# Layer 0 of a two-layer graph network: row sums taken inside the weighted sums, a scatter moved behind the gathers, and layer-norm statistics shared between VectorE and ScalarE

## The chip, the core and the metric

The kernel runs on one core of a Trainium2 chip. A core has five engines that run side by side, each from its own queue of instructions: TensorE (PE, matrix products; its weight loads are listed as PEld), VectorE (DVE), ScalarE (ACT), GpSimd (POOL, which here also issues the indirect DMAs) and SyncE (SP, which issues plain DMAs). The metric is the time of the whole program on the device in microseconds, lower is better.

## The reference

Inputs are 2708 nodes with 1024 features, a 0/1 adjacency matrix and square weights. Cut to what matters:

```python
# layer 0
f, g = x @ Wf + bf, x @ Wg + bg
e    = relu(f @ g.T)
att  = softmax(where(adj > 0, e, -9e15), axis=1)
x    = layernorm(x + att @ (x @ W + bW))
# layer 1
h    = x @ W1
e    = leaky_relu(h @ a1 + (h @ a2).T, 0.2)
att  = softmax(where(adj > 0, e, -9e15), axis=1)
x    = layernorm(x + relu(att @ h))
# layernorm(x) = (x - mean) / sqrt(var + 1e-5), over the 1024 features
```

The adjacency has some 16 neighbours a node, so the kernel never forms a full attention matrix.

## The kernel before

**Preparation (to about 250 us).** The adjacency is read row by row, each row's neighbours are turned into a list of at most 40 indices, and the nodes are sorted by list length into 85 groups of 32. A block is four groups (128 nodes; the first holds one group only). Each node has its list split over four partitions, so that one *tile* is 128 gathered rows: one neighbour for each of four list quarters of 32 nodes. Most blocks of layer 0 have 20 tiles. The products `M = Wf Wg^T` and the vectors derived from the biases are made here, so that a score is one dot product of a neighbour's raw row of x with the row `F = x M + c` of the node.

**Layer 0 (about 250 to 1155 us)** is one loop over blocks, software-pipelined over five of them: while block k is summed, block k+1 is scored, block k+2 gets its `F`, the block before k is multiplied by W, and block k+3 is loaded. In the order in which the loop body emits them, the steps are:

- `replicate(b, k)`: four ScalarE copies spread 32 rows of `F` from PSUM to the 128 partitions of one of four `Fr` buffers; each block needs four of these, sixteen copies of 32x1024.
- `q_dot` (the bias part of the score) and the steps of `close` of the block before: residual sum `z = pm + z`, statistics, `z` normalized in place by one ScalarE instruction, `z` written to `X1S`, two dots of `z` with `u2b` and `u1b`, and `z` with its dot scattered into the table `T1`, which layer 1 gathers from.
- `Layer.sums`: `po += st^T ring`, where `ring` holds the gathered rows and `st` the attention weights. Four column strips of TensorE work at once, one queue of matmuls each. A tile's two halves of 512 columns lie in different strips. When both have been emitted, its ring slot is free and the next gather is emitted on POOL (`gathers`). The ring has 20 slots. The row sums of the softmax are a small matmul of `rs` into a PSUM tile `pt`, of which VectorE takes the reciprocal `ri`; ScalarE scales `po` by it into `y`.
- `x_turn` (transposes of a later block's x), the product with `Wt`, `q_spread`, the product with `M`, and the transposes of `y`. All transposes and the row sums share two rotating `pt` buffers, the products share two `pm` buffers.
- `dots` (one VectorE pass of 1024 columns per tile), then `soft`, which makes `st` and `rs`.

**What sets the order.** Each engine is wrapped in `InOrder`: its instructions are issued exactly in the order in which the loop emits them, and wait for other engines by semaphores. Generators (`close`, `turn`, `q_spread`) are advanced by `next` at chosen places, which is how a step's pieces are interleaved; `hooks` in `sums` let the caller run the rest of `close` after the thirteenth tile. Since all calls go through one wrapper, nearly every line of the profile is that wrapper's, L71; steps are told apart by tile names. The tile called `xT` serves for the transposed y too, and a group `j<-ring,Fr` is one dot.

**Layer 1** gathers rows of `T1`, sums them first, multiplies by `W1`, and closes with the same `norm`.

Of the kernel before, what the change touches and what calls it, by code (L numbers as in the profile page):

```python
# [8 lines left out]
F32 = mybir.dt.float32  # L9
BF16 = mybir.dt.bfloat16  # L10
I32 = mybir.dt.int32
# [95 lines left out]
def listed_path(ctx, tc, x, adj, Wf, bf, Wg, bg, W, bW, W1, a1, a2, out):  # L107
# [39 lines left out]
    make_identity(nc, ident)  # L147
    ones = const.tile([P, 1], F32, name="ones")
    nc.gpsimd.memset(ones, 1.0)
    ones3 = const.tile([35, P], BF16, name="ones3")  # L150
    nc.gpsimd.memset(ones3, 1.0)

    stack = const.tile([P, 32], F32, name="stack")
    rep = const.tile([P, Q, 32], F32, name="rep")
# [16 lines left out]
    f1 = const.tile([P, NB], F32, name="f1")  # L171
    nc.gpsimd.memset(f1, 0.0)
    s0 = const.tile([P, 1], F32, name="s0")
    rows3 = const.tile([35, D], BF16, name="rows3")
    c3, b3 = rows3[0:3], rows3[32:35]
    scores = [const.tile([P, Q, QT], F32, name=f"scores{i}") for i in range(2)]
    for t in scores:
# [357 lines left out]
    def product(n, xT, w, row=None):  # L535


        pm = ps_m.tile([P, H, 512], F32, name="pm")
        for h in range(H):
            half_product(pm, h, n, xT, w, row)  # L540
        return pm

    def half_product(pm, h, n, xT, w, row=None):
        c = slice(h * 512, (h + 1) * 512)
        if row is not None:
            pe.matmul(pm[:n, h, :], ones3[row:row + 3, :n], rows3[row:row + 3, c], start=True, stop=False)
        for k in range(KC):
            pe.matmul(pm[:n, h, :], xT[:, k, :n], w[:, k, c],
                      start=(row is None and k == 0), stop=(k == KC - 1))

    def two_products(n, xT, w, row=None):

        halves = [ps_m.tile([P, H, 512], F32, name="pm") for h in range(H)]
        for h in range(H):
            half_product(halves[h], h, n, xT, w, row)
        return halves

    def split_product(xT, w, parts, row=None, pm=None):

        pm = ps_m.tile([P, H, 512], F32, name="pm") if pm is None else pm
        for h in range(H):
            c = slice(h * 512, (h + 1) * 512)
            if row is not None:
                pe.matmul(pm[:32, h, :], ones3[row:row + 3, :32], rows3[row:row + 3, c], start=True, stop=False)
            for k in range(KC // Q):
                for p in range(Q):
                    i = p * KC // Q + k
                    pe.matmul(pm[32 * p:32 * p + 32, h, :], xT[:, i, :32], w[:, i, c],  # L570
                              start=(k == 0 and (row is None or p > 0)), stop=(k + 1 == KC // Q))
        yield
        act.copy(parts, flat(pm))
        yield
        pm = ps_m.tile([P, H, 512], F32, name="pm")
        for h in range(H):
            pe.matmul(pm[:, h, :], rep, parts[:, h * 512:(h + 1) * 512], start=True, stop=True)
        return pm
# [11 lines left out]
    def scatter(table, idx, src):  # L590
        pool.indirect_dma_start(
            out=table, out_offset=bass.IndirectOffsetOnAxis(ap=idx, axis=0), in_=src,
            in_offset=None, bounds_check=N - 1, oob_is_err=False)

    def norm(z, n, made=None):


        st = small.tile([P, H, 6], F32, name="bst")
        mv = small.tile([P, 2], F32, name="mv")
        for h in range(H):  # L600
            if made is not None:
                made(h)
            dve.bn_stats(st[:n, h, :], z[:n, h * 512:(h + 1) * 512])
        dve.bn_aggr(mv[:n], st[:n])
        var, r, t = (small.tile([P, 1], F32, name=s) for s in ("var", "rstd", "newton"))
        dve.tensor_scalar(var[:n], mv[:n, 1:2], EPS, None, op0=ALU.add)
        ri, ti = r.bitcast(I32), t.bitcast(I32)
        dve.tensor_scalar(ti[:n], var.bitcast(I32)[:n], 1, None, op0=ALU.logical_shift_right)
        dve.tensor_scalar(ri[:n], ti[:n], -1.0, float(0x5F3759DF), op0=ALU.mult, op1=ALU.add)
        for _ in range(3):  # L610
            dve.tensor_scalar(t[:n], var[:n], r[:n], r[:n], op0=ALU.mult, op1=ALU.mult)
            dve.tensor_scalar(t[:n], t[:n], -0.5, 1.5, op0=ALU.mult, op1=ALU.add)
            dve.tensor_scalar(r[:n], r[:n], t[:n], None, op0=ALU.mult)
        sh = small.tile([P, 1], F32, name="sh")
        dve.tensor_scalar(sh[:n], mv[:n, 0:1], r[:n], -1.0, op0=ALU.mult, op1=ALU.mult)
        yield
        act.activation(z[:n, :D], z[:n, :D], AF.Identity, bias=sh[:n], scale=r[:n])
# [24 lines left out]
    class Layer:  # L642
# [57 lines left out]
            u.rs = small.tile([P, Q], F32, name="rs")  # L700
            dve.tensor_reduce(u.rs[:, :u.G], sc, AX.X, ALU.add)

        def sums(self, u, po, hooks, y):

            pt = ps_t.tile([P, 4, P], F32, name="pt")
            place = lambda k, h: 32 * ((k + 2 * h) % 4)
            for h in range(H):  # L710
                for k in range(u.G):
                    j = place(k, h)
                    pe.matmul(pt[j:j + 32, 0, h:h + 1], stack, u.rs[:, k:k + 1], start=True, stop=True)
            ri = small.tile([P, H], F32, name="ri")
            spans = [(slice(0, P), slice(0, H))] if u.G == 4 else \
                [(slice(j, j + 32), slice(h, h + 1)) for h in range(H) for j in (place(0, h),)]
            for rows, h in spans:
                dve.reciprocal(ri[rows, h], pt[rows, 0, h])
            index = {(k, t): m for m, (k, g, t) in enumerate(u.tiles)}

            queues = []
            for c in range(4):
                two = [(k, h) for h, k in enumerate((c, (c + 2) % 4)) if k < u.G]
                queues.append([(k, h, t) for t in range(u.T) for k, h in two if t < TILES[u.gs[k]]])
            done, halves = 0, {}
            while any(queues):
                now = [q.pop(0) for q in queues if q]
                for k, h, t in now:
                    j = place(k, h)
                    pe.matmul(po[j:j + 32, h, :], u.st[:, u.col[k, t], :],  # L730
                              self.rows(u.at + index[k, t])[:, h * 512:(h + 1) * 512],
                              start=(t == 0), stop=(t == TILES[u.gs[k]] - 1))
                for k, h, t in now:
                    halves[k, t] = halves.get((k, t), 0) + 1
                    if halves[k, t] == H:
                        self.free.add(u.at + index[k, t])
                        self.gathers()
                        for f in hooks.get(done, []):
                            f()
                        done += 1  # L740
            for k, fs in sorted(hooks.items()):
                if k >= done:
                    for f in fs:
                        f()
            for h in range(H):
                rows = slice(0, P) if u.G == 4 else slice(place(0, h), place(0, h) + 32)
                c = slice(h * 512, (h + 1) * 512)
                act.activation(y[rows, c], po[rows, h, :], AF.Copy, scale=ri[rows, h:h + 1])
# [107 lines left out]
    with ExitStack() as s0s:  # L856
# [62 lines left out]
        def close(b):  # L919
# [6 lines left out]
                dve.tensor_add(z[:n, c], pm[h][:n, h, :], z[:n, c])  # L926

            if b + 1 < NB:
                dve.tensor_add(z[:n, :D], flat(pm)[:n], z[:n, :D])
            steps = norm(z, n, None if b + 1 < NB else add)  # L930
            next(steps)
            yield
            for _ in steps:
                pass
            sp.dma_start(X1S[start[b]:start[b] + m, :], z[:m, :D])
            yield
            dot(z[:n, :D], u2b, n, z[:n, D:D + 1])
            dot(z[:n, :D], u1b, n, f1[:n, b:b + 1])
            yield
# [72 lines left out]
        for k, u in enumerate(units):  # L1012
# [9 lines left out]
                for _ in yTs[back][1]:  # L1022
                    pass
            reps = list(range(len(nxt.gs))) if nxt is not None and not first else []
            for r in reps[:1]:
                replicate(nxt.b, r)
            next(closing, None)
            if loaded is not None:
                q_dot(loaded)
                loaded = None  # L1030
            next(closing, None)
            for r in reps[1:3]:
                replicate(nxt.b, r)
            if nxt is None:

                for _ in closing:
                    pass
                Wp[back] = product(P, yTs.pop(back)[0], Wt, 32)
            lay.sums(u, po, {12: [lambda s=closing: [None for _ in s]]}, y[b])
            closing = iter(())  # L1040
            if ahead is not None and not first:
                x_turn(ahead)
# [3 lines left out]
            if back is not None and nxt is not None:  # L1046
                load_residual(back)
                if back > 0:
                    Wp[back] = product(P, yTs.pop(back)[0], Wt, 32)
                else:  # L1050
                    Wp[back] = whole(split_product(yTs.pop(back)[0], Wt, frp.tile([P, D], F32, name="Fr"), 32))
            if k + 2 == NB:
                load_residual(b)
            spreading = iter(())
# [16 lines left out]
            if k + 4 < NB and not first:  # L1071
                load_lists(seq[k + 4])
            if nxt is not None:
                dots(nxt, 0, len(nxt.tiles))
            for _ in spreading:
                pass
            if nxt is not None:
# [5 lines left out]
        load_residual(b)  # L1083
        for _ in yTs[b][1]:
            pass
        Wp[b] = two_products(P, yTs.pop(b)[0], Wt, 32)
        for _ in closing:
            pass
        for _ in close(b):
# [521 lines left out]
```

## Time and profile before

| | us |
|---|---|
| median of 3 runs | 1772.31 (1768.69 to 1783.73) |
| the profiled execution, its own time | 1778.06 |
| its span from first to last instruction | 1776.3 |
| PE busy | 1586.4 (89%) |
| DVE busy | 1295.3 (73%) |
| POOL busy | 1188.0 (67%) |
| ACT busy | 643.4 (36%) |
| mean granted TensorE clock | 0.959 |

Every number of a view belongs to the one profiled execution. A line of the timeline gives start, duration (of several merged instructions, from the first's start to the last's end), engine, source line, operation, output<-input names with shapes, and a count; in brackets stands the idle time just before it and what ended that idle time. A mean clock below 1.00 in a stretch is a TensorE that ran part of it at reduced speed. An engine's busy share says little by itself: an engine may be busy because it is the bound, or idle because something in front of it in its own queue waits.

### The profile page before, as it was taken

Reading aid. Unit: us, or ns where it says so; the run is one execution under the profiler, and the core shown is the slowest. Engines: PE = TensorE matmul, PEld = TensorE weight load, DVE = VectorE, ACT = ScalarE, POOL = GpSimd, SP = SyncE. Lnnn points to the kernel's source line nnn. Section 1 sums busy time; section 2 is a strip of 40 time slices with the busy share of each in tenths; the row PEclk is TensorE's granted clock in tenths of the full one; section 3 lists DMA queues with packets and bytes.
Section 4 is the critical chain, followed back from the end, with each engine's and each line's share of the span. In section 5 each row is a group of like instructions: output and inputs, shape, how many; then the busy total and the mean of one; then the engine's idle time right before and its main releaser. Section 6 shows DMA issues by size and latency. Waiting matters only on the chain. (4 is left out here: it accounts for less than half of the span.)

```text
span 1776.3 us, 22882 instructions
## 1 busy us (share of the span) xinstructions
PE 1586.4 (89%) x6969; PEld 677.2 (38%) x6969; DVE 1295.3 (73%) x4262; ACT 643.4 (36%) x902; POOL 1188.0 (67%) x1192
## 2 busy tenths in 40 slices
PE   5999389899999999999999999739899897998896
PEld 3444133343444443443444444313344333343342
DVE  5879756888888888888888887637656556665652
ACT  4545454444444455454555554101111111111111
POOL 8878476467666666667666664167777777777740
PEclk9999789899999999999999999969999999999998
DMA  7646168568777777777787787299999999999960
GB/s 284 245 160 240 44 227 318 207 213 289 291 283 270 264 250 256 272 282 266 277 295 278 268 296 297 88 359 368 365 369 394 392 392 378 383 395 391 391 250 37
DMA packets 149984, 502.79 MB, mean 283 GB/s; under 512 B 32340, under 2 KB 32372, under 8 KB 147144
## 3 DMA queue, kind: packets, MB, share of 16 engines
q0 software_dynamic: 132032, 428.29, 65.3%
q1 hardware_dynamic: 10202, 55.72, 8.4%
q10 hardware_dynamic: 7618, 17.23, 2.7%
q8 instruction: 57, 0.93, 0.2%
q14 instruction: 75, 0.61, 0.1%
HBM read 509.64 MB, written 33.75 MB: 306 GB/s over the span
## 5 line engine op out<-in xcount | busy, mean ns | idle before, releaser
L71 POOL DMA_INDIRECT ring<-in_x_dram,SL x405 | 438.6, 1083 | 253.1 <-issue 91.4
L71 DVE SCALAR_TENSOR_TENSOR j<-ring,Fr 128x1024 bf16<-128x1024 f32 x402 | 494.4, 1230 | 82.5 <-DMA ring<-in_x_dram,SL 55.7
L71 PE MATMUL po<-ring,st 128*32 128x512 f32 x2616 | 322.7, 618 | 47.8 <-ACT y L71 30.4
L71 ACT COPY Fr<-pm 32x1024 f32<-32x1024 f32 (+2 forms) x353 | 340.7, 965 | 21.1 <-PE pm L71 16.4
L71 PE MATMUL pm<-M,yT 128*128 128x512 f32 (+1 forms) x704 | 313.3, 598 | 0.5 <-ACT yT L71 0.5
L71 PE MATMUL pm<-M,xT 128*128 128x512 f32 x672 | 307.2, 611 | 0.0
L71 PE MATMUL pm<-Wt,xT 128*128 128x512 f32 (+1 forms) x704 | 303.5, 599 | 0.0
L71 POOL DMA_INDIRECT ring<-T,SL x249 | 246.9, 992 | 83.3 <-issue 69.9
L71 ACT ACTIVATE scores<-scores 128x12 f32<-128x12 f32 (+9 forms) x65 | 14.0, 216 | 669.3 <-DVE scores L71 669.3
L71 PEld LDWEIGHTS pm<-M,yT 128*128 128x128 f32 (+1 forms) x704 | 127.8, 186 | 184.7 <-issue 183.5
L71 PEld LDWEIGHTS pm<-M,xT 128*128 128x128 f32 x672 | 127.1, 194 | 165.3 <-issue 165.3
L71 PEld LDWEIGHTS po<-ring,st 128*32 128x32 f32 x2616 | 103.8, 114 | 222.9 <-issue 182.3
L71 POOL DMA_INDIRECT more<-T,SL x156 | 154.7, 992 | 47.5 <-issue 40.7
L71 PEld LDWEIGHTS pm<-Wt,xT 128*128 128x128 f32 (+1 forms) x704 | 125.0, 186 | 151.8 <-issue 151.1
L409 POOL TENSOR_TENSOR adj<-adj,iota 128x2708 f32<-128x2708 f32 (+3 forms) x23 | 130.5, 5685 | 24.4 <-ACT adj L71 24.3
L412 DVE MAX8 cand<-adj 128x8 f32<-128x136 f32 (+2 forms) x440 | 97.2, 285 | 35.8 <-POOL adj L409 35.8
L71 PE MATMUL pm<-halfT,WfT 128*128 128x512 f32 x256 | 113.2, 597 | 1.1 <-ACT WfT L71 1.1
L71 POOL DMA_INDIRECT SL<-LD,idq x85 | 86.0, 1011 | 25.8 <-issue 22.4
L71 PE MATMUL po<-more,st 128*32 128x512 f32 x624 | 83.8, 632 | 17.8 <-ACT y L71 17.8
L71 DVE TENSOR_SCALAR scores<-ring,f1q 128x4 f32<-128x4 f32 (+6 forms) x69 | 16.0, 238 | 99.3 <-DMA ring<-T,SL 95.9
L71 PEld LDWEIGHTS pm<-halfT,WfT 128*128 128x128 f32 x256 | 48.0, 192 | 57.4 <-issue 54.7
L71 ACT ACTIVATE y<-po,ri 128x512 f32<-128x512 f32 (+1 forms) x88 | 57.5, 678 | 20.9 <-PE po L71 20.3
(211 smaller groups left out, 1509.0 us busy)
## 6 DMA issues: line engine op xcount, KB each, us to landing
adj<-in_adj_dram SPq DMA_DIRECT2D x21, 1354.0 KB
X1S<-z SPq DMA_DIRECT2D x19, 512.0 KB
ring<-in_x_dram,SL POOLq DMA_INDIRECT x405, 6.6
rows<-in_L_gnn_Wg_dram ACTq DMA_DIRECT2D x8, 512.0 KB
rows<-in_L_gnn_Wf_dram ACTq DMA_DIRECT2D x8, 512.0 KB
rows<-in_L_gnn_W_dram ACTq DMA_DIRECT2D x8, 512.0 KB
Wt<-in_L_gnn_W_dram ACTq DMA_DIRECT2D x1, 4096.0 KB
M<-in_L_gnn_W_dram SPq DMA_DIRECT2D x1, 4096.0 KB
```

The source lines that it names most:

```text
L71: made = self.tc.keep_in_program_order(op(*args, **kwargs))
L409: nc.gpsimd.tensor_tensor(k[:n, cut], k[:n, cut], iota[:n, cut], op=ALU.mult)
L412: nc.vector.max(cand[:n, s, :], k[:n, s * SEG:min((s + 1) * SEG, N)])
```

## The change

Five things change in layer 0, and one of them (the root) in layer 1 as well.

1. *Bias rows.* The bias enters a product as a first matmul. Its operands grow from 3 rows to 128: `rows3` has all 128 partitions, cleared to zero outside the six rows in use, and the constant operand is a column of `pick`, broadcast. The bias matmuls of both halves are emitted ahead of both halves' products.
2. *Row sums within sums.* The matmul of the row sums is emitted after the first four finished tiles, the reciprocal after the last. Two of the four strip queues take their two halves in reverse order.
3. *Scatter behind the gathers.* `hooks` is gone. The rest of `close`, now the scatter alone, is emitted after `sums` and after the first five dots of the next block.
4. *Statistics.* The residual sum also gives the sum of each row (`accum_out`); ScalarE's Square with the mean as its bias gives the sum of squares; `bn_stats` and `bn_aggr` remain for the last block of layer 0 and for layer 1. `rsqrt` has two VectorE operations in a Newton step instead of three.
5. *Order.* The `next(closing)` calls are placed anew around `replicate` and `q_dot`: two `replicate` calls instead of one now stand between the first and the second.

```diff
-    ones3 = const.tile([35, P], BF16, name="ones3")
-    nc.gpsimd.memset(ones3, 1.0)
+    pick = const.tile([P, 2], BF16, name="pick")
+    nc.gpsimd.memset(pick, 0.0)
+    nc.gpsimd.memset(pick[0:3, 0:1], 1.0)
+    nc.gpsimd.memset(pick[32:35, 1:2], 1.0)
...
-    rows3 = const.tile([35, D], BF16, name="rows3")
+    rows3 = const.tile([P, D], BF16, name="rows3")
+    nc.gpsimd.memset(rows3, 0.0)
...
         for h in range(H):
+            bias_row(pm, h, n, row)
+        for h in range(H):
             half_product(pm, h, n, xT, w, row)
         return pm
 
+    def bias_row(pm, h, n, row):
+        pe.matmul(pm[:n, h, :], pick[:, row:row + 1].to_broadcast([P, n]), rows3[:, h * 512:(h + 1) * 512], start=True, stop=False)
...
-        if row is not None:
-            pe.matmul(pm[:n, h, :], ones3[row:row + 3, :n], rows3[row:row + 3, c], start=True, stop=False)
...
+    def rsqrt(v, n, scale):
+        half, r, t = (small.tile([P, 1], F32, name=s) for s in ("half", "rstd", "newton"))
+        dve.tensor_scalar(half[:n], v, 0.5 * scale, 0.5 * EPS, op0=ALU.mult, op1=ALU.add)
+        ri, ti = r.bitcast(I32), t.bitcast(I32)
+        dve.tensor_scalar(ti[:n], half.bitcast(I32)[:n], 1, None, op0=ALU.logical_shift_right)
+        dve.tensor_scalar(ri[:n], ti[:n], -1.0, float(0x5F3759DF - 0x400000 - (1 << 31)), op0=ALU.mult, op1=ALU.add)
+        for _ in range(3):
+            dve.tensor_scalar(t[:n], half[:n], r[:n], r[:n], op0=ALU.mult, op1=ALU.mult)
+            dve.tensor_scalar(r[:n], t[:n], 1.5, r[:n], op0=ALU.subtract, op1=ALU.mult)
+        return r
...
-        def sums(self, u, po, hooks, y):
-            pt = ps_t.tile([P, 4, P], F32, name="pt")
+        def sums(self, u, po, y):
             place = lambda k, h: 32 * ((k + 2 * h) % 4)
-            for h in range(H):
-                for k in range(u.G):
-                    j = place(k, h)
-                    pe.matmul(pt[j:j + 32, 0, h:h + 1], stack, u.rs[:, k:k + 1], start=True, stop=True)
-            ri = small.tile([P, H], F32, name="ri")
...
+            def totals():
+                pt = ps_t.tile([P, 4, P], F32, name="pt")
+                for h in range(H):
+                    for k in range(u.G):
+                        j = place(k, h)
+                        pe.matmul(pt[j:j + 32, 0, h:h + 1], stack, u.rs[:, k:k + 1], start=True, stop=True)
+                return pt
...
                 two = [(k, h) for h, k in enumerate((c, (c + 2) % 4)) if k < u.G]
+                if c > 1:
+                    two.reverse()
...
             while any(queues):
+                if pt is None and done >= min(4, u.T):
+                    pt = totals()
...
-                        for f in hooks.get(done, []):
-                            f()
                         done += 1
...
+            if pt is None:
+                pt = totals()
+            ri = small.tile([P, H], F32, name="ri")
...
             if b + 1 < NB:
-                dve.tensor_add(z[:n, :D], flat(pm)[:n], z[:n, :D])
-            steps = norm(z, n, None if b + 1 < NB else add)
-            next(steps)
-            yield
-            for _ in steps:
-                pass
+                mean, ss, sh = (small.tile([P, 1], F32, name=s) for s in ("mean", "ss", "sh"))
+                dve.scalar_tensor_tensor(z[:n, :D], flat(pm)[:n], 1.0, z[:n, :D], op0=ALU.mult, op1=ALU.add,
+                                         accum_out=mean[:n])
+                dve.tensor_scalar(mean[:n], mean[:n], -1.0 / D, None, op0=ALU.mult)
+                yield
+                act.activation(flat(pm)[:n], z[:n, :D], AF.Square, bias=mean[:n], accum_out=ss[:n])
+                yield
+                r = rsqrt(ss[:n], n, 1.0 / D)
+                dve.tensor_scalar(sh[:n], mean[:n], r[:n], None, op0=ALU.mult)
+                yield
+                act.activation(z[:n, :D], z[:n, :D], AF.Identity, bias=sh[:n], scale=r[:n])
...
             sp.dma_start(X1S[start[b]:start[b] + m, :], z[:m, :D])
-            yield
             dot(z[:n, :D], u2b, n, z[:n, D:D + 1])
             dot(z[:n, :D], u1b, n, f1[:n, b:b + 1])
             yield
...
-            for r in reps[:1]:
+            next(closing, None)
+            for r in reps[:2]:
                 replicate(nxt.b, r)
-            next(closing, None)
             if loaded is not None:
                 q_dot(loaded)
                 loaded = None
             next(closing, None)
-            for r in reps[1:3]:
+            next(closing, None)
+            for r in reps[2:3]:
                 replicate(nxt.b, r)
...
-            lay.sums(u, po, {12: [lambda s=closing: [None for _ in s]]}, y[b])
+            lay.sums(u, po, y[b])
+            early = min(5, len(nxt.tiles)) if nxt is not None else 0
+            if nxt is not None and not first:
+                dots(nxt, 0, early)
+            else:
+                early = 0
+            for _ in closing:
+                pass
...
             if nxt is not None:
-                dots(nxt, 0, len(nxt.tiles))
+                dots(nxt, early, len(nxt.tiles))
```

## The prediction

> **What bounds the kernel now.** I read the windows first, to find the stretch that the diff touches. Layer 0's steady blocks run from 369.2 to 1083.5 us:
>
> ```profile
> 369.20:1083.50 714.30, 690.94 (x3082) 293.64 (x3082) 623.50 (x1404) 353.05 (x426) 477.81 (x446) 1.00 0.76 271
> ```
>
> Columns: PE, PEld, DVE, ACT, POOL busy us, granted clock, DMA share, GB/s. TensorE is busy for 97% of it at full clock. The stretch holds 17 blocks, 42.0 us each. Then the timeline of one block by engine, TensorE first:
>
> ```profile
> 661.20 1.04 PE L71 MATMUL pt<-ident,y 128*128 128x128 f32 x8
> 664.17 0.29 PE L71 MATMUL pt<-rs,stack 128*32 128x1 f32 x14 [1.94 <-ACT xT L71]
> ...
> 664.33 8.76 PE L71 MATMUL po<-ring,st 128*32 128x512 f32 x79
> 673.02 1.37 PE L71 MATMUL pt<-ident,xb 128*128 128x128 f32 x8
> 674.32 0.39 PE L71 MATMUL pm<-rows,ones 3*128 3x512 bf16 x1
> ```
>
> The order is y's transposes, row sums, weighted sums, x's transposes, the W product, the M product. TensorE pauses once, 1.94 us ahead of the row sums. Over 400 to 1000 us the waits list 12.0 us (8 times, for ACT xT) and 8.4 us (6 times, for DVE rs) there: 20.4/14 = 1.5 us a block. So about 40.6 us is TensorE's own floor. Now ScalarE and VectorE in the same block:
>
> ```profile
> 662.79 0.22 ACT L71 ACTIVATE scores<-scores 128x24 f32<-128x24 f32 x1 [19.91 <-DVE scores L71]
> 663.04 1.14 ACT L71 COPY xT<-pt 128x512 f32<-128x512 f32 x3
> 664.05 4.04 ACT L71 COPY Fr<-pm 32x1024 f32<-32x1024 f32 x4
> 669.82 1.24 ACT L71 ACTIVATE z<-z,sh,rstd 128x1024 f32<-128x1024 f32 x1 [1.73 <-DVE sh L71]
> 671.09 8.12 ACT L71 COPY Fr<-pm 32x1024 f32<-32x1024 f32 x8
> ```
> ```profile
> 663.94 1.21 DVE L71 TENSOR_TENSOR z<-pm,z 128x1024 f32<-128x1024 f32 x1
> ...
> 669.57 0.21 DVE L71 TENSOR_SCALAR sh<-mv,rstd 128x1 f32<-128x1 f32 x1
> 669.70 1.22 DVE L71 SCALAR_TENSOR_TENSOR j<-xb,rb 128x1024 bf16<-128x1024 f32 x1
> ...
> 671.10 1.22 DVE L71 SCALAR_TENSOR_TENSOR j<-z,u2b 128x1024 bf16<-128x1024 f32 x1
> ...
> 673.51 0.16 DVE L71 RECIPROCAL ri<-pt 128x2 f32<-128x2 f32 x1
> 673.63 1.22 DVE L71 SCALAR_TENSOR_TENSOR j<-ring,Fr 128x1024 bf16<-128x1024 f32 x1
> ```
>
> z is normalized behind four Fr copies, eight follow. The reciprocal sits behind the two dots over z. x's second four transposes need the PSUM buffer that it frees (two pt buffers rotate): 673.51 lets the bias matmul start at 674.32, 0.81 later. Who waits for ri is small today:
>
> ```profile
>   PEld pt L71: 6.5, 16
> ```
>
> The reciprocal lands just as the sums end. That is the tight joint of this schedule.
>
> **What the Trainium skill says.** "TensorE: Matmul & The Clock Gate", section "Architectural detail", calls ScalarE and VectorE strict FIFOs. The trace agrees: at 671.10 the dot starts 0.04 us after z ends, and the dots over ring follow it only. The same page, "What's actually happening", says that idleness in a free-running window of 3413 ns halves the array's clock. The trace shows both outcomes after short pauses: 2.10 us before 707.01 was followed by
>
> ```profile
> 708.00:712.00 4.00, 4.00 (x32) 1.28 (x27) 3.55 (x14) 2.76 (x3) 0.99 (x1) 0.66 0.02 4
> ```
>
> (clock 0.66, sums of 10.46 instead of 8.76 us); 3.11 us before 835.45 was not. "ScalarE: Activation LUTs", section "Table sets", warns that a function outside the loaded set costs a load; this trace has one load of 1.283 us in all, and Square is not in it.
>
> **The change, part by part.** I write E for the end of y's transposes and R for the start of the reciprocal. By the compiled instruction order, ScalarE's new order is Exp, three y copies, Square, *eight* Fr copies, z, four Fr copies, y. VectorE's is sum-add, mean, q dot, root, two dots over z, reciprocal, dots over ring. So "dots first" does not put the ring's dots ahead of z's, and z moves from behind four copies to behind eight.
>
> *From R to the next E (TensorE).* Today 0.81 to the bias, then 674.32 to 704.91 = 30.59 for both products and y's transposes: 31.4 us. Bias rows: each takes 0.32 us start to start (631.65 to 631.97), four a block. With 128 rows and loads grouped by product I bound them between -0.4 and +0.4 us a block, from 128x128 loads at 0.19 against 0.09 us on one side and hidden loads on the other; I take -0.2. E = R + 31.2.
>
> *From E to the next R (ScalarE, then VectorE).* Copies of yT end 0.8 after E (619.93+1.04 against 620.62+1.14). Square: like z, 1.24, plus an accumulator read of 0.19 (the row of adj): 1.43. Writing to PSUM may make it 1.0 to 1.3; I keep 1.24. Eight copies 8.12. z 1.24 and two hops, 1.3. The two dots 2.42 (628.43 to 630.85). Sum 0.8+1.43+8.12+1.3+2.42 = 14.1.
>
> Period 31.2 + 14.1 = 45.3 us. The row sums no longer hold the weighted sums, but those end well inside the 14.1: 9.1 with the totals, 0.7 for half of x's transposes, then TensorE waits 14.1 + 0.3 - 9.8 = 4.6 us, *in every block*. That is longer than the clock's window. One window at half clock loses at most 1.7 us of products directly on this path; part of the window falls in the pause. I take 1.4, ends 0 and 3.4. Period 46.7.
>
> *VectorE's own loop* is shorter: 20 dots x 1.272 = 25.4, soft 3.9, sum-add with its read and mean 1.6, then Square to R without the y copies 13.3 plus the reciprocal and a hop 0.2: 44.4. Either loop alone is over 42.
>
> *Statistics.* From z's sum to sh is 4.6 us on VectorE now (665.16 to 669.78). New: 0.1 read, 0.2 mean, three setup operations 0.56, six Newton operations of 0.31, sh 0.2 = 2.9; 1.7 us saved, but it ends about seven us before z's turn on ScalarE. Worth nothing while the copies stand in front; without them it would come back as 1.7 a block. Layer 1's root saves 0.4 on its last block only.
>
> *Gathers.* Reversing two of the four queues finishes tiles 0 and 1 after one round (0.85 us) instead of two, so the first gather comes 0.85 earlier; the scatter (1.3 us of POOL) no longer stands among them. VectorE waits 52.5 us for ring DMAs in layer 0 (65 times), about 3 a block; those go. Covered: dots start at E + 14.3, and gather m lands at E + 1.2 + 1.35m + 6.7, always earlier.
>
> *The scatter behind the gathers* stands before xb, z and four SL loads on POOL. Twenty gathers end at E + 28.2; scatter landing takes 8.2 us, and the residual z, in the same buffer, waits for it, then issues and lands in 5.9: E + 43.6 with the issue gaps. The sum-add needs it by E + 46.0 to keep Square behind the y copies. Hidden by 2.4 us; in a 43 us block it would be next in line. SL loads end by E + 44, before the next gathers.
>
> *Start.* Clearing rows3 on POOL is at most 1 us (128x484 f32 took 0.49), and POOL idles 2.02 us at 8.7: nothing. *The first and last blocks:* the first reciprocal moves from 334.5 to 340.3 by the same sum, but TensorE waits there for Fr copies anyway, leaving 2.1 us at the next E and R at 385.1 instead of 377.3: +7.8. Sixteen periods to 1051.8 (42.15 now): 16 x (46.7 - 42.15) = +72.8. To the next sums +0.8. At the end the last reciprocal but one delays y by 2.5. Layer 1 (1159.7 to the end) keeps its 616.6 us.
>
> Sum: 7.8 + 72.8 + 0.8 + 2.5 = +84 us. Against its own run the profiled time 1778.1 (span 1776.3) becomes 1862. The median of runs, 1772.3, is 0.3% under that execution: **1856 us**.
>
> **The rivals.**
> (a) *The stall without the clock loss.* Period 45.3: 7.8 + 50.4 + 3.3 = +62, 1834. For it: the 3.11 us pause left the clock alone. Against: 4.6 us can't miss a window as those did.
> (b) *Faster.* ScalarE's queue is not what ends last: the copies of Fr finish early enough, the reciprocal comes by the end of the sums, and TensorE's pause of 1.5 us vanishes. Decides where E to R falls under 9.8. 17 x 1.5 + 17 x 0.2 = -29: 1743. For it: 97% busy and a pause that goes. Against: eight copies alone are 8.12.
> (c) *No difference,* 1772: what the copies add and the vanished DMA waits cancel, were the TensorE wait hidden by a changed rotation of buffers. The compiled order keeps VectorE's wait on x's second transposes.
> (d) *Worse still.* Square displaces Exp's set: two loads of 1.28 us a block (2.66 each by the skill's section "What ACT_TABLE_LOAD costs"), on ScalarE's part of the path: 17 x 2.6 to 17 x 5.3, +44 to +90 more, 1900 to 1946. Its main evidence against is that Identity, Copy, Relu and Exp already share one load.
>
> **How the numbers follow.** Main case 0.58, (a) 0.24, (b) 0.06, (c) 0.04, (d) 0.08. Faster or slower by 1% (18 us) is about what this measurement can tell. Main case with its ends: bias +-0.4 and clock 0.8 to 2.2 a block give 1840 to 1875; with (a) and its bias bound the low end is 1825, and a part of (d) or a second clock window takes the high end to 1882. (b), (c) and most of (d) stay outside. Slower 0.90, same 0.04, faster 0.06.
>
> **What would show it.** Reciprocals 46.7 us apart; TensorE waiting 4 to 5 us for ri before x's second transposes in each block; clock below 1.00 after it; the dot over z waiting 6 us or more for ACT z; no DVE wait for ring DMAs; scatter after the twentieth gather; layer 1 as long as before. I am wrong if z's Identity runs ahead of the copies, if x's transposes don't wait, or if a table load stands beside Square.

## The result and the profile after

The changed kernel takes 1849.05 us (median of 4 runs, 1846.37 to 1851.21); the kernel before, run beside it, 1773.95 (4 runs). The ratio is 1.040, with a 95% interval from 1.037 to 1.043 (the two medians alone give 1.042). The profiled execution took 1847.13 us, with a span of 1845.3 against 1776.3 before: 69.0 us more.

The steady stretch of layer 0 again, in the same window of time as before (PE, PEld, DVE, ACT, POOL busy us, clock, DMA share, GB/s):

```profile
369.20:1083.50 714.30, 643.77 (x2806) 281.42 (x2799) 550.10 (x1209) 346.00 (x425) 437.55 (x423) 0.94 0.70 253
```

TensorE's busy time in it has dropped from 690.94 to 643.77 us, and the clock from full to 0.94. The timeline of two blocks on TensorE, with the weighted sums left out, shows both losses:

```profile
696.21 0.66 PE L71 MATMUL pt<-ident,xb 128*128 128x128 f32 x4
701.21 1.01 PE L71 MATMUL pt<-ident,xb 128*128 128x128 f32 x4 [4.34 <-DVE ri L71]
702.01 1.06 PE L71 MATMUL pm<-rows,pick 128*128 128x512 bf16 x2
702.87 14.85 PE L71 MATMUL pm<-Wt,xT 128*128 128x512 f32 x32
717.55 0.28 PE L71 MATMUL pt<-qd,rep 128*128 128x4 f32 x2
717.69 0.59 PE L71 MATMUL pm<-rows,pick 128*128 128x512 bf16 x2
718.12 13.89 PE L71 MATMUL pm<-M,xT 128*128 128x512 f32 x32
731.86 1.04 PE L71 MATMUL pt<-ident,y 128*128 128x128 f32 x8
...
746.68 1.11 PE L71 MATMUL pt<-ident,xb 128*128 128x128 f32 x4 [4.35 <-DVE ri L71]
747.58 1.06 PE L71 MATMUL pm<-rows,pick 128*128 128x512 bf16 x2
748.44 15.95 PE L71 MATMUL pm<-Wt,xT 128*128 128x512 f32 x32
```

Between the halves of x's transposes TensorE now waits 4.3 us for the reciprocal. The product behind the pause takes 14.85 us in one block and 15.95 in the next, where the M product, undisturbed, takes 13.89. The windows behind the two pauses give the reason in the clock column:

```profile
702.00:704.00 2.00, 2.00 (x6) 1.09 (x4) 1.93 (x5) 1.97 (x4) 1.43 (x2) 0.50 0.99 393
704.00:706.00 2.00, 2.00 (x5) 0.76 (x5) 1.97 (x3) 1.98 (x4) 1.55 (x2) 0.80 1.05 400
706.00:708.00 2.00, 2.00 (x6) 0.92 (x5) 1.93 (x5) 1.98 (x3) 1.54 (x2) 1.00 1.01 334
...
748.00:750.00 2.00, 2.00 (x4) 1.01 (x3) 1.97 (x3) 1.98 (x5) 1.70 (x2) 0.50 1.04 424
750.00:752.00 2.00, 2.00 (x4) 0.82 (x3) 1.93 (x5) 1.98 (x3) 1.39 (x3) 0.50 1.05 414
752.00:754.00 2.00, 2.00 (x6) 0.83 (x5) 1.97 (x3) 1.98 (x3) 1.61 (x2) 0.86 1.00 401
```

Half speed lasts to about 705 in the first block and to about 753 in the second. Why the reciprocal is late stands in the queues of ScalarE and VectorE of that block:

```profile
732.49 1.14 ACT L71 COPY xT<-pt 128x512 f32<-128x512 f32 x3 [2.69 <-PE pt L71]
733.50 1.15 ACT L71 ACTIVATE pm<-z,mean 128x1024 f32<-128x1024 f32 x1
...
734.65 8.09 ACT L71 COPY Fr<-pm 32x1024 f32<-32x1024 f32 x8
742.77 1.24 ACT L71 ACTIVATE z<-z,sh,rstd 128x1024 f32<-128x1024 f32 x1
```
```profile
737.04 0.21 DVE L71 TENSOR_SCALAR sh<-mean,rstd 128x1 f32<-128x1 f32 x1
744.04 1.23 DVE L71 SCALAR_TENSOR_TENSOR j<-z,u2b 128x1024 bf16<-128x1024 f32 x1 [6.78 <-ACT z L71]
...
746.46 0.17 DVE L71 RECIPROCAL ri<-pt 128x2 f32<-128x2 f32 x1
```

The statistics are ready at 737.25. z runs at 742.77, behind eight copies, and VectorE stands still for 6.78 us with the two dots over z and the reciprocal behind them. The steps between y's transposes and the reciprocal thus take 13.56 us (732.90 to 746.46). In the whole run, TensorE's weight loads wait for the reciprocals 4.6 us (14 times) in the kernel before. (The 6.5 us that the prediction shows are from a view that also lists waits for the scaling of y, which reads `ri`.) In the changed kernel the total and the number of waits are

```profile
  PEld pt L71: 82.5, 18
```

Layer 0's first gather for layer 1 comes at 1228.6 us instead of 1159.7, 68.9 later; layer 1 takes 616.7 us, as before.

### The profile page after: what moved, and what is told of

Read it like the earlier page. It is cut to its first block, busy times and chain, and to the rows that moved or that the text cites. A ratio compares the mean times of both kernels' runs of the same rounds, so it can differ in the third digit from the quotient of the medians.

```text
span 1845.3 us, 22970 instructions
## 1 busy us (share of the span) xinstructions
PE 1598.2 (87%) x6969; PEld 691.6 (37%) x6969; DVE 1252.2 (68%) x4109; ACT 667.5 (36%) x944; POOL 1175.3 (64%) x1195
## 5 line engine op out<-in xcount | busy, mean ns | idle before, releaser
L71 POOL DMA_INDIRECT ring<-in_x_dram,SL x405 | 416.7, 1029 | 253.0 <-PE po L71 111.4
L71 PE MATMUL pm<-Wt,xT 128*128 128x512 f32 (+1 forms) x704 | 325.1, 637 | 4.2 <-DMA Wt<-in_L_gnn_W_dram 4.2
L71 PE MATMUL pm<-M,xT 128*128 128x512 f32 x672 | 295.8, 599 | 0.0
L71 PEld LDWEIGHTS pm<-Wt,xT 128*128 128x128 f32 (+1 forms) x704 | 142.5, 206 | 183.5 <-issue 176.0
L71 POOL DMA_INDIRECT more<-T,SL x156 | 155.1, 994 | 49.0 <-issue 44.4
L71 PEld LDWEIGHTS po<-ring,st 128*32 128x32 f32 x2616 | 94.6, 113 | 221.8 <-issue 177.3
L71 DVE SCALAR_TENSOR_TENSOR j<-z,u2b 128x1024 bf16<-128x1024 f32 (+1 forms) x20 | 24.5, 1225 | 130.4 <-ACT z L71 130.4
L71 PE MATMUL pt<-ident,xb 128*128 128x128 f32 x168 | 35.0, 348 | 86.0 <-DVE ri L71 78.2
L71 POOL DMA_INDIRECT z<-in_x_dram,ids x21 | 30.3, 1445 | 94.4 <-DVE j L71 72.0
```

The source lines that it names most:

```text
L71: made = self.tc.keep_in_program_order(op(*args, **kwargs))
```

## The experiments

Theory: the loss is the place of z on ScalarE, behind eight `Fr` copies. It delays z's dots, these delay the reciprocal, TensorE waits for it in every block and its clock falls. Rivals: the loss comes from other parts of the change (the statistics, the place of the scatter, the bias rows), or the clock has no share in it. Every ratio below is against the kernel before on the same chip. It took 1774.5 us beside four of the kernels (four copies ahead of z, the filled pause, the reciprocal ahead of the dots, the bias rows) and 1774.9 us beside the other four.

### Four copies ahead of z instead of eight, in the changed kernel

```diff
-            for r in reps[:2]:
+            for r in reps[:1]:
                 replicate(nxt.b, r)
...
-            for r in reps[2:3]:
+            for r in reps[1:3]:
                 replicate(nxt.b, r)
```

> The changed kernel with one replicate call (four Fr copies) instead of two between Square and z; the other eight copies follow z. My theory (z's place in ScalarE's queue delays the reciprocal, and that holds TensorE): E to R falls from 13.6 to 9.5 us, under the 9.8 us of sums and half of x's transposes, so TensorE's wait for ri and the half clock after it vanish; the period falls from 46.0 to about 41 us and the time from 1849 to about 1764 us, under the kernel before. Rival (the residual z, loaded after the scatter, is next in line): period about 43, time about 1798 us. Rival (another of the five edits makes it slow): time stays over 1830 us.

Measured: 1753.63 us (1750.76 to 1760.97), ratio 0.989 (0.986 to 0.993). With all other parts of the change in place, this one edit takes back 95 us and is faster than the kernel before: the interval stays below 1. One block of its timeline, TensorE, then ScalarE:

```profile
658.22 0.66 PE L71 MATMUL pt<-ident,xb 128*128 128x128 f32 x4
659.96 0.66 PE L71 MATMUL pt<-ident,xb 128*128 128x128 f32 x4 [1.09 <-DVE ri L71]
660.46 0.38 PE L71 MATMUL pm<-rows,pick 128*128 128x512 bf16 x1
660.89 13.90 PE L71 MATMUL pm<-Wt,xT 128*128 128x512 f32 x32
```
```profile
650.86 1.12 ACT L71 ACTIVATE pm<-z,mean 128x1024 f32<-128x1024 f32 x1 [0.68 <-DVE mean L71]
...
652.00 4.02 ACT L71 COPY Fr<-pm 32x1024 f32<-32x1024 f32 x4
656.05 1.24 ACT L71 ACTIVATE z<-z,sh,rstd 128x1024 f32<-128x1024 f32 x1
```

TensorE waits 1.09 us, and the product behind it runs at full speed (13.90). The wait was expected to vanish; from 400 to 1000 us it still comes in each of 15 blocks and sums to 19.4 us, since the reciprocal follows y's transposes by some 10.6 us and not by 9.5. The half clock has gone: the mean in that stretch is 1.00. The reciprocals are 40.8 us apart (374.03 to 1068.17 in 17 steps), as forecast.

Where the 21 us under the kernel before come from is read from the trace and not tested by itself. From the reciprocal to the end of y's transposes a block now takes 30.2 us, where the kernel before takes 31.4; some 1.0 us of that lies in the two products with their bias rows. TensorE's pause ahead of the row sums (20.4 us from 400 to 1000 us in the kernel before) has gone too, but the 19.4 us of waiting for `ri` stand in its place.

### Eight copies ahead of z, in the kernel before

```diff
-            for r in reps[:1]:
+            for r in reps[:2]:
                 replicate(nxt.b, r)
...
-            for r in reps[1:3]:
+            for r in reps[2:3]:
                 replicate(nxt.b, r)
```

> The same kernel as before_eight, on another chip, since the times there can't be set beside the other experiments. Theory (the eight copies that stand ahead of z make the loss): all copies of a product ahead of z in the kernel before puts about 4 us more in front of each reciprocal, the wait of TensorE for the reciprocal grows to about 4 us and its clock falls: 1810 to 1825 us, which is most of the loss of the changed kernel. Rival (the loss needs the other parts of the change): within 1% of the kernel before, 1760 to 1785 us.

Measured: 1844.26 us (1843.57 to 1847.76), ratio 1.039 (1.036 to 1.042). The edit alone makes a kernel as slow as the whole change (1.040). The theory holds in direction, but its forecast, 1810 to 1825 us, was too low. Two pieces of TensorE's timeline in it:

```profile
701.06 0.98 PE L71 MATMUL pt<-ident,xb 128*128 128x128 f32 x4 [2.91 <-DVE ri L71]
701.97 0.60 PE L71 MATMUL pm<-rows,ones 3*128 3x512 bf16 x1
702.50 8.19 PE L71 MATMUL pm<-Wt,xT 128*128 128x512 f32 x16
...
718.12 0.38 PE L71 MATMUL pm<-rows,ones 3*128 3x512 bf16 x1
718.43 7.13 PE L71 MATMUL pm<-M,xT 128*128 128x512 f32 x16
725.50 0.38 PE L71 MATMUL pm<-rows,ones 3*128 3x512 bf16 x1
725.82 7.13 PE L71 MATMUL pm<-M,xT 128*128 128x512 f32 x16
732.78 1.04 PE L71 MATMUL pt<-ident,y 128*128 128x128 f32 x8
```

A pause of 2.9 us was enough to halve the clock too: half a product takes 8.19 instead of 7.13, and the mean clock from 702 to 704 us is 0.50. The reciprocals are 46.1 us apart (378.28 to 1069.52 in 15 steps), the changed kernel's 46.0. The other parts cancel in this chain. Without Square the reciprocal comes 12.5 us after y's transposes (733.82 to 746.32) instead of 13.6 (732.90 to 746.46), and with the old bias rows the M product with its bias takes 14.66 us (718.12 to 732.78) instead of 14.17, which is 1.0 us for the two products of a block.

### TensorE kept busy in the pause

x's first four transposes are repeated seven more times, with the same values; this is extra work, and nothing else differs from the changed kernel.

```diff
-            for k in range(4):
-                pe.transpose(pt[:, k, :n], rows[at, (k0 + k) * P:(k0 + k + 1) * P], ident[at, at])
+            for i in range(1 + (fill if k0 == 0 else 0)):
+                for k in range(4):
+                    pe.transpose(pt[:, k, :n], rows[at, (k0 + k) * P:(k0 + k + 1) * P], ident[at, at])
...
-                x_turn(ahead)
+                x_turn(ahead, 7)
```

> The changed kernel with the first four transposes of x repeated seven more times (about 4.5 us of TensorE work that writes the same values), so that TensorE is busy in the pause ahead of the reciprocal. Theory (the pause costs clock besides itself): clock 1.00 in the steady blocks, the two products take 30.5 us from the reciprocal instead of 31.9 to 33.1, period about 44.2, time about 1820 us. Rival (the clock does not matter on this path): no change or slower than 1849 us.

Measured: 1815.94 us (1813.35 to 1817.07), ratio 1.023 (1.021 to 1.026). Useless work makes the changed kernel 33 us faster. One pause of it on TensorE, and the steady window:

```profile
507.15 3.71 PE L71 MATMUL pt<-ident,xb 128*128 128x128 f32 x32
512.52 0.66 PE L71 MATMUL pt<-ident,xb 128*128 128x128 f32 x4 [1.65 <-DVE ri L71]
513.01 0.38 PE L71 MATMUL pm<-rows,pick 128*128 128x512 bf16 x1
513.44 13.90 PE L71 MATMUL pm<-Wt,xT 128*128 128x512 f32 x32
```
```profile
369.20:1083.50 714.30, 686.92 (x3404) 327.75 (x3412) 563.79 (x1251) 359.76 (x441) 454.02 (x435) 1.00 0.73 262
```

The reciprocal is no earlier than in the changed kernel (13.6 to 14.2 us after y's transposes, against 13.6); only the clock is back (1.00 against 0.94). So of the 75 us lost at least 33 are the clock, and the rest is mainly the wait itself. Rival (a) of the prediction, a stall without a clock loss, describes this kernel (1834 us forecast, 1816 measured) and not the changed one.

### The reciprocal ahead of z's two dots

```diff
             sp.dma_start(X1S[start[b]:start[b] + m, :], z[:m, :D])
+            yield
             dot(z[:n, :D], u2b, n, z[:n, D:D + 1])
...
             lay.sums(u, po, y[b])
+            next(closing, None)
```

> The changed kernel with the two dots over z emitted after the reciprocal instead of ahead of it; z stays behind eight copies. My theory: TensorE no longer waits for ri, but VectorE still waits for z, and its own loop (20 dots, soft, sum-add, Square, eight copies, z, two dots) takes 44.3 us. So about 1.7 us a block comes back of the 3.9 lost: about 1820 us. Rival (the loss is all in TensorE's wait): back to about 1775 us. Rival (all in VectorE's wait): stays at 1849 us.

Measured: 1806.44 us (1802.45 to 1808.00), ratio 1.018 (1.016 to 1.021), a better time than expected. TensorE's wait for the reciprocal is gone. VectorE's waits for z remain, since z still stands behind eight copies and the dots over it wait for it all the same. TensorE waits on VectorE one step further on (waits from 400 to 1000 us: total, times, longest):

```profile
DVE j L71 <- ACT z L71: 94.3, 14, 6.7
...
PE po L71 <- DVE st L71: 39.1, 14, 3.1
```

The reciprocals are 44.1 us apart (370.36 to 1031.25 in 15 steps). That fits the second loop of the prediction, VectorE's own, which it put at 44.4; the agreement of the two figures is the evidence.

### The bias rows alone, in the kernel before

```diff
-    ones3 = const.tile([35, P], BF16, name="ones3")
+    pick = const.tile([P, 2], BF16, name="pick")
...
-    rows3 = const.tile([35, D], BF16, name="rows3")
+    rows3 = const.tile([P, D], BF16, name="rows3")
+    nc.gpsimd.memset(rows3, 0.0)
...
         for h in range(H):
+            bias_row(pm, h, n, row)
+        for h in range(H):
             half_product(pm, h, n, xT, w, row)
```

> The kernel before with the bias rows alone changed (128 rows, both halves' bias first). By the trace of the changed kernel each product with its bias takes 14.2 instead of 14.7 us. Theory (in the kernel before VectorE and the gathers set the period and TensorE waits 1.5 us a block): TensorE waits 1 us more instead, and the time falls by 1 to 6 us, mostly ahead of the steady blocks: about 1770 us. Rival (TensorE sets the period): 18 blocks of 1.0 us, about 1755 us.

Measured: 1780.58 us (20 runs), ratio 1.004 (1.002 to 1.005): a miss, slower where a gain was expected. From 400 to 1000 us TensorE is busy for 565.0 us instead of 579.0. It reaches the end of its products earlier and finds the other engines where they were, so it waits longer ahead of the row sums. In the kernel before these waits were 12.0 and 8.4 us; now they are

```profile
PE pt L71 <- ACT xT L71: 20.8, 8, 3.1
PE pt L71 <- DVE rs L71: 12.8, 6, 3.3
```

In some blocks the longer pause costs the clock as well; the mean of the stretch falls from 1.00 to 0.98. A block with this loss (clock 0.50 from 493 to 495 us), and the next without:

```profile
493.00 0.39 PE L71 MATMUL pt<-rs,stack 128*32 128x1 f32 x16 [3.11 <-ACT xT L71]
493.21 10.35 PE L71 MATMUL po<-ring,st 128*32 128x512 f32 x80
...
535.47 0.29 PE L71 MATMUL pt<-rs,stack 128*32 128x1 f32 x14 [1.55 <-ACT xT L71]
...
535.63 8.76 PE L71 MATMUL po<-ring,st 128*32 128x512 f32 x79
```

That the lost clock outweighs the saved work is read from this trace; no run fills the pauses of this kernel.

### The other parts, once z stands behind four copies

Three kernels start from the one with four copies ahead of z (1753.63). They and the eight copies in the kernel before also ran on another chip, on which the kernel before itself took 1929 us. Those times (1875.66, 1913.55, 1896.24 and 1984.77 us, in the order reciprocal, scatter, statistics, eight copies) can't be set beside the others and are not used here.

*The reciprocal ahead of the dots*, by the edit shown above.

> The changed kernel with four copies ahead of z and the reciprocal ahead of z's two dots. Theory A (after the first repair only about 1 us of TensorE's wait per block is left, and the gathers come next in line): 1745 to 1755 us, no measurable difference to z_after_four's 1753.6. Theory B (the reciprocal still sets the period): about 1 us of each of 18 blocks comes back, 1733 us.

Measured: 1748.00 us (1747.00 to 1750.81), ratio 0.985 (0.982 to 0.988). The time lies where theory A put it, and the interval overlaps that of the four copies alone (0.986 to 0.993). From 400 to 1000 us TensorE's 19.4 us of waiting for ri become 21.7 us of waiting for st.

*The scatter in the middle of the sums.*

```diff
                         self.gathers()
+                        if done == 12:
+                            for _ in rest:
+                                pass
                         done += 1
...
-            lay.sums(u, po, y[b])
+            lay.sums(u, po, y[b], closing)
```

> The changed kernel with four copies ahead of z and z's closing part (dots, reciprocal, scatter) put back into the middle of the sums, after 12 of the gathered groups, as the kernel before has the scatter. Theory A (the scatter behind the gathers is what makes the next gathers about 1 us late): equal or up to 1% faster, 1740 to 1754 us. Theory B (the reciprocal then comes later and TensorE waits for it): slower, 1765 us or more.

Measured: 1757.45 us (1755.04 to 1763.14), ratio 0.990 (0.986 to 0.994). The edit moves the scatter alone; the dots over z and the reciprocal keep their places, although the expectation names them too. The time lies between the two theories (1740 to 1754 us, and 1765 or more). The ratio can't be told from that of the four copies alone (0.989), so where the scatter stands is worth nothing that these runs show. With the scatter behind the gathers, the load of the residual, which comes behind it, stands still for 49.5 us from 400 to 1000 us. The profile puts these waits down to VectorE's dots; that it is really the scatter's landing is read from the order, since the load fills the buffer that the scatter reads. With the scatter in the middle these waits are gone. Instead GpSimd is early and stands ahead of the first gather of a block until the sums have begun (73.6 us, of which the profile puts 52.0 down to VectorE's mean and 21.6 to the sums themselves). One wait has taken the place of the other.

*The statistics of the kernel before* (`bn_stats`, `bn_aggr`), with the shorter root.

```diff
-                dve.scalar_tensor_tensor(z[:n, :D], flat(pm)[:n], 1.0, z[:n, :D], op0=ALU.mult, op1=ALU.add,
-                                         accum_out=mean[:n])
-                dve.tensor_scalar(mean[:n], mean[:n], -1.0 / D, None, op0=ALU.mult)
+                dve.tensor_add(z[:n, :D], flat(pm)[:n], z[:n, :D])
+                steps = norm(z, n)
+                next(steps)
                 yield
-                act.activation(flat(pm)[:n], z[:n, :D], AF.Square, bias=mean[:n], accum_out=ss[:n])
...
-                r = rsqrt(ss[:n], n, 1.0 / D)
-                dve.tensor_scalar(sh[:n], mean[:n], r[:n], None, op0=ALU.mult)
...
-                act.activation(z[:n, :D], z[:n, :D], AF.Identity, bias=sh[:n], scale=r[:n])
+                for _ in steps:
+                    pass
```

> The changed kernel with four copies ahead of z and with the statistics of the kernel before (VectorE's two statistics instructions per block and their gathering, in place of the summing residual add and ScalarE's squares). Theory A (the statistics are worth nothing to the time): 1750 to 1758 us, as z_after_four. Theory B (z comes later by what the older statistics take longer, about 1.4 us in each of 18 blocks): about 1778 us.

Measured: 1743.78 us (1742.27 to 1745.63), ratio 0.982 (0.979 to 0.985), the fastest kernel of this study and faster than both theories gave. The new statistics don't help. If anything they cost about 10 us: the two intervals (0.979 to 0.985, and 0.986 to 0.993) don't overlap, though the two kernels ran on different chips. TensorE's and ScalarE's waits from 400 to 1000 us in the kernel with the old statistics are

```profile
ACT z L71 <- DVE sh L71: 21.2, 14, 2.2
...
PE po L71 <- DVE st L71: 9.0, 11, 1.7
PE pt L71 <- DVE ri L71: 5.7, 10, 1.4
```

With the new ones TensorE waits 19.4 us for `ri` and 1.8 for `st`, and ScalarE waits 15.0 us for the mean, ahead of Square, and never for `sh`. So TensorE waits 6.5 us less over 15 blocks with the old statistics, and the reciprocals are 40.4 instead of 40.8 us apart. A likely reason is that Square (1.12 us, behind a wait of 0.68) stands ahead of the four copies in ScalarE's queue, while `bn_stats` on VectorE runs beside them. No run separates Square from the summing add or from the place of the root, so that stays argued. The row sums within the sums and the reversed queues have no run of their own either.

## Why the prediction was right

It forecast 1856 us in a range from 1825 to 1882, and the time was 1849. The mechanism was the one described: TensorE's loop and VectorE's own both over 42 us, z behind eight copies, a wait of 4 to 5 us for ri in every block (4.3), a clock under 1.00 behind it, VectorE waiting over 6 us for z (6.8), no wait for ring DMAs left. Placing the copies alone reproduced it, and undoing that alone removed it. Below, R is the start of the reciprocal and E the end of y's transposes, as in the prediction. By its terms:

- *From R to E:* predicted 31.2, of which the bias rows -0.2 within a bound of 0.4 either way. At full clock the changed order takes 30.2, read in the kernel with the filled pause (600.60 to 630.82); the kernel before takes 31.4. The M product with its bias takes 14.17 instead of 14.66 us, and the W product is of the same size, so the rows save 1.0 a block and the bound was broken. It priced a bias matmul by its own start-to-start time and not by what it does to the products behind it: a half's 16 matmuls took 7.13 us behind a 3-row bias, and a pair of halves takes 13.89.
- *From E to R:* predicted 14.1, measured 13.56. Square started 0.6 after E, where 0.8 was counted for y's copies, and held ScalarE for 1.15 and not 1.43: its accumulator read hid behind the next copy.
- *Clock:* predicted 1.4 us a block within 0 to 3.4. In the changed kernel R to E takes 31.9 and 33.1 us in turn, so the half clock costs about 1.7 and 2.9, or 2.3 on average. The prediction counted one stretch of half clock of at most 1.7; every other block lost more. Its reason was a pause longer than the clock's window. Pauses of 2.9 us in the kernel before with eight copies cost about as much (33.0 and 34.2 instead of 31.4), while one of 3.11 us in the kernel before cost nothing, so the length of a pause alone doesn't decide it. What does, no run shows.
- *Period:* predicted 46.7, measured 46.0. The terms were off by -1.0, -0.5 and +0.9, which partly cancelled: that the period came out this close is in part luck.
- *First blocks:* predicted +7.8, measured +1.8 (379.09 against 377.30). This term was wrong. It kept the head of layer 0 as it was and moved the first reciprocal from 334.5 to 340.3. But the first transposes of y came at 281.43 instead of 286.46, and that reciprocal fell at 334.91.
- *Steady blocks:* predicted +72.8, measured +61.5 (735.98 against 674.48 us for sixteen periods).
- *Tail:* predicted +3.3, measured +5.6 from the reciprocal of the last steady block to layer 1.

The sum is 1.8 + 61.5 + 5.6 = 68.9 us, where 84 was forecast. That the median came within 0.4% is luck as well: the forecast was scaled down by 0.3%, since the profiled execution of the kernel before lay above its median, while that of the changed kernel (1847.13) lay below its own.

*Statistics* were called worth nothing while the copies stand in front, and 1.7 us a block without them. The first held: sh was ready 5.5 us before z ran. The second is not borne out: with four copies still ahead the old statistics are not slower, though ScalarE then waits 21.2 us for `sh` from 400 to 1000 us; no run has z ahead of all copies. *The scatter* was called hidden, and next in line in a 43 us block. Hidden it was: in the steady stretch of the changed kernel the residual sum never waits for its load. At 40.8 us a block the residual sum does wait for it, in 9 of 15 blocks, though for 2.8 us in all; putting the scatter back gave no time that could be measured. *Table loads* (rival d): the changed kernel has one load in all, ahead of an adjacency row as before, and none at Square. *Faster* (rival b) is what the change becomes with the copies in their old order, though by 21 us and not 29, and with a wait for `ri` in place of the pause that went. *No difference* (rival c) needed a wait that the compiled order didn't remove.

## What to carry to other kernels

When a change regroups calls for one engine, write out the new order of that engine's queue, and ask of every instruction moved back which engine waits for its result and what is queued behind that waiter; here four copies of 1.0 us made an edit of several parts 4% slower, and without them the same edit is 1% faster. Look at the clock behind a pause of TensorE as well as at its length, and test the clock's share by filling the pause. A saving on one engine that ends in a wait for another may cost time instead of giving none, so try the parts of a change alone.

## What the runs showed that I had not expected

- Useless transposes made a kernel faster: 1849 us became 1816 when the pause of 4.3 us was filled with 28 more.
- Behind pauses of 4.34 and 4.35 us the half clock lasted to about 704.8 in one block and to about 752.6 in the next, by the mean clock of the windows; that is 3.6 and 5.9 us from the end of the pause. It also followed pauses of 2.91 us and of 3.11 us, but not the pause of 3.11 us that the prediction quotes.
- Bias matmuls of 3 rows, one ahead of each half, cost more than 128-row ones ahead of both. The pair of halves with their bias rows takes 14.66 us with 3 rows between the halves and 14.17 with 128 rows ahead of both. The runs don't separate the number of rows from the order.
- A kernel with 1.0 us of TensorE work less in each of its blocks came out 0.4% slower (0.2 to 0.5%).
